# Loading the first group's keys, queries and values amid the projections, and later groups' keys and values in parts

## The chip, the cores and the metric

The kernel runs on one core of one Trainium2 chip. The metric is the device time of one execution in microseconds (us); lower is better. The core has five engines with a queue of their own: PE (TensorE, matmuls), DVE (VectorE), ACT (ScalarE), POOL (GpSimd) and SP (SyncE, which here only issues DMA requests). DMA requests are carried out by 16 DMA engines.

## The reference

Two layers on a graph with 2708 nodes and 128 features. The first layer is an attention with 128 "dimensions" d, each with its own 2708 x 2708 score matrix of inner size 8; the adjacency matrix is added twice to the scores. The second layer is a two-step graph convolution. Both are followed by a residual addition and a layer norm.

```python
q = (x @ Wq.T).reshape(d, n, h)          # d = 128, n = 2708, h = 8
k = (x @ Wk.T).reshape(d, n, h)
v = (x @ Wv.T).reshape(d, n, h)
a = einsum('dnh,dmh->dnm', q, k) * d**-0.5 + adj + adj
out = einsum('dnm,dmh->dnh', softmax(a, axis=2), v).reshape(n, h * d) @ Wo.T
x = layernorm(x + out)
hid = adj @ (x @ W2) + b2
x = layernorm(x + adj @ (hid @ W4) + b4 + hid @ res_w.T + res_b)
```

## The kernel before

The work has three stages, one after the other.

**Projections** (lines 179 to 210). The 2708 rows of x go in 22 chunks `MC` of 128 (the last has 20). For each chunk and each of k, q, v, PE makes a 128 x 1024 product in PSUM (`pp`). ACT copies it to an SBUF tile, for k and q as a rounded high part (`pr`, pool of 4), and DVE adds the low part (line 206) and two reductions for a later range test (line 210). SP then stores the tile into DRAM: `ks` and `qs` (line 208, 1 MB each, in runs of 512 bytes) and `vs` (line 201, 0.5 MB). The reshape of the reference makes one of the 128 dimensions a run of 2708 positions in these DRAM tensors; so the loop reads back from DRAM what the projections wrote. The inputs are requested in the order x, weights of k, q, v (lines 185 and 189).

**Attention loop** (lines 213 to 443). The 128 dimensions go in 32 groups of `GB` = 4. A group needs:

- its keys: `load_keys` (line 276) makes 16 requests of 8 rows of 2708 numbers each (84.6 KB) into `k_raw`, which has one buffer; `order_keys` (line 286) has POOL put them in order in 8 casts (line 291) and 4 small ones (line 295), into a tile with two buffers;
- its values: `load_values` (line 297) makes 4 requests for `v_raw` and 4 small ones for `v_short`; `spread_values` (line 306) has POOL spread them in 4 copies;
- its queries, by block of 452 columns: `load_q` (line 310), 8 requests.

Each group runs over 6 blocks `QBS` of query columns, and each block over 9 steps of a `plan`. A step makes its scores on PE (`score`, line 350), DVE adds an adjacency tile to them (`add_near`, line 357), and ACT takes the exponential of the step's 4 to 8 score tiles at once (line 443). For nine of the key chunks, the exponential of the adjacency is multiplied on POOL instead of added (lines 440 and 441). PE sums exponentials times values into `acc` (`add_up`, line 371). When a block's sum is complete, DVE copies it and SP stores it (`hand_on`, lines 377 and 379).

Adjacency tiles come from DRAM on SP's queue (`load_adj`, line 319): `col` (pool of 9), `two` (a pair of chunks, pool of 3) and `ecol` (exponentials, pool of 7; in group 0 ACT makes them on line 338 and SP stores them on line 339). At each step's beginning the program asks for what is needed up to `ahead` = 8 loads beyond that step.

The order of all this is written out by hand: the generator `interleave` yields pieces, sums and hand-overs, and `tc.manual_schedule()` keeps that order on every engine's queue. The projections lie ahead of the manual schedule; there the order follows from the framework's scheduler. SP's queue is strict: a request that waits (for a buffer, or for data) holds up all that come after it. What asks for a next group's data is these lines:

```python
if (b, i) == (1, 0):
    load_keys(g + 1)
elif (b, i) == (2, 0):
    load_values(g + 1)
elif b > 1 and n % 2:
    h = ((b - 2) * len(plan) + i) // 2     # order_keys(g+1, h), then spread_values
```

For group 0, all of it stands ahead of the loop (lines 385 to 391): `load_keys(0)`, `load_values(0)`, `load_q(0, 0)`, then `order_keys` and `spread_values`. The tiles of the loop lie in SBUF where the projections' tiles were.

**The rest** (from line 446): output projection, layer norm, the range test and the graph convolution. The change does not touch it.

Of the kernel before, what the change touches and what calls it, by code (L numbers as in the profile page):

```python
# [9 lines left out]
F32 = mybir.dt.float32  # L10
# [8 lines left out]
P = 128  # L19
H = 8  # L20
# [109 lines left out]
def graph_attention_gcn(ctx: ExitStack, tc: tile.TileContext, x, xT, adj, adjT, adjP, adjS,  # L130
# [46 lines left out]

    with ExitStack() as s:
        wpool = s.enter_context(tc.tile_pool(name="wqkv", bufs=1))
        sb = s.enter_context(tc.tile_pool(name="proj", bufs=4))  # L180
        ps = s.enter_context(tc.tile_pool(name="ps_proj", bufs=4, space=PSUM))

        xT_sb = wpool.tile([P, N], F32, name="xT_sb")
        for i0, mi in ((0, P), (P, N - P)):
            nc.sync.dma_start(xT_sb[:, ds(i0, mi)], xT[:, ds(i0, mi)])
        w_sb = []
        for name, w in (("k", WkT), ("q", WqT), ("v", WvT)):
            t = wpool.tile([P, H * P], F32, name=f"w{name}_sb")
            nc.sync.dma_start(t, w)
            w_sb.append(t)  # L190
        v3 = vs.rearrange("(i g) e -> i (g e)", g=P)
        for c, (i0, mi) in enumerate(MC):
            for w, dst in zip(w_sb, (ks, qs, vs)):
                pp = ps.tile([P, 2, 512], F32, tag="pp", name="pp")
                for h in range(2):
                    nc.tensor.matmul(pp[:mi, h, :], xT_sb[:, ds(i0, mi)], w[:, ts(h, 512)], start=True, stop=True)
                flat = pp[:mi].rearrange("p a b -> p (a b)")
                if dst is vs:
                    o = sb.tile([P, H * P], F32, tag="po", name="po")
                    nc.scalar.copy(o[:mi], flat)  # L200
                    nc.sync.dma_start(v3[ds(i0, mi)], o[:mi])
                else:
                    f = half_scale if dst is qs else 1.0
                    o = sb.tile([P, 2, H * P], F32R, tag="pr", name="pr")
                    nc.scalar.mul(o[:mi, 0], flat, f)  # L205
                    nc.vector.scalar_tensor_tensor(o[:mi, 1], flat, f, o[:mi, 0].bitcast(F32), ALU.mult, ALU.subtract)
                    d3 = dst.rearrange("e (i g) -> i e g", g=P)
                    nc.sync.dma_start(d3[ds(i0, mi)], o[:mi].bitcast(F32).rearrange("p l (e g) -> p (l e) g", g=P))
                    for i, op in enumerate((ALU.max, ALU.min)):
                        nc.vector.tensor_reduce(ends[:mi, int(dst is qs), i, c : c + 1], o[:mi, 0].bitcast(F32), AX.X, op)  # L210


    with ExitStack() as s:
# [7 lines left out]
        epool = s.enter_context(tc.tile_pool(name="weights", bufs=4))  # L221
        ppool = s.enter_context(tc.tile_pool(name="products", bufs=4))
        opool = s.enter_context(tc.tile_pool(name="sums", bufs=2))
        ps = s.enter_context(tc.tile_pool(name="ps_s", bufs=2, space=PSUM))
        pq = s.enter_context(tc.tile_pool(name="ps_q", bufs=1, space=PSUM))
        pa = s.enter_context(tc.tile_pool(name="ps_a", bufs=1, space=PSUM))
# [49 lines left out]
        def load_keys(g):  # L276

            t = raw.tile([P, N], F32R, tag="k_raw", name="k_raw")
            for j in range(GB):
                r0 = (GB * g + j) * N  # L280
                for i in range(4):
                    nc.sync.dma_start(t[ds(32 * j + H * i, H), :].bitcast(F32), ks[ds(H * (i // 2), H), ds(r0, N)])
            groups[g] = kpool.tile([P, NU, P], F32R, tag="k", name="k"), k_short[g % 2], vals[g % 2], v_short[g % 2]
            raw_keys[g] = t
# [12 lines left out]
        def load_values(g):  # L297
            t = raw.tile([P, GB, NU * H], F32, tag="v_raw", name="v_raw")
            vz = v_short[g % 2]
            for j in range(GB):  # L300
                r0 = (GB * g + j) * N
                nc.sync.dma_start(t[:, j, :], vs[ds(r0, P * NU), :].rearrange("(p c) e -> p (c e)", c=NU))
                nc.sync.dma_start(vz[ds(32 * j, SHORT), ds(VW * j, H)], vs[ds(r0 + P * NU, SHORT), :])
            values[g] = t
# [14 lines left out]
        def load_adj(n):  # L319
# [6 lines left out]
            elif m < 0 and g > 0:  # L326
                t = exp_cols[g, b, -1 - m] = ecols.tile([P, QB], F32, tag="ecol", name="ecol")
                nc.sync.dma_start(t[:, :nw], near_exp[b, -1 - m][:, :nw])
            else:
                t = adj_cols[g, b, m] = cols.tile([P, QB], F32, tag="col", name="col")  # L330
                m = -1 - m if m < 0 else m
                nc.sync.dma_start(t[:, :nw], adjP[ds(m * P, P), ds(n0, nw)])

# [50 lines left out]
        ahead, loaded = 8, 0  # L384
        load_keys(0)
        load_values(0)
        load_q(0, 0)
        for h in range(9):
            order_keys(0, h)
        for j in range(GB):  # L390
            spread_values(0, j)
        for what, n, c, beside in interleave(plan, len(steps) // len(plan), NU):
# [10 lines left out]
            if c == 0:  # L403
# [4 lines left out]
                if g + 1 < NG:  # L408
                    if (b, i) == (1, 0):
# [302 lines left out]
```

## Time and profile before

| | |
|---|---|
| median of 3 runs | 7141.34 us (7120.3 to 7145.82) |
| profiled execution: time | 7152.27 us |
| profiled execution: span from first to last instruction | 7150.5 us |
| mean granted TensorE clock | 0.981 |
| busy: PE, DVE, ACT, POOL | 95%, 86%, 92%, 80% |
| last projection store has landed, first key request | 204.74 us |
| ACT's first large exponential of the loop | 238.17 us |

The profile is of one execution. Busy time is the time in which an engine has an instruction of the program in work; the DMA share is the mean busy share of the 16 DMA engines. Times are microseconds from the first instruction, and L443 means line 443 of the kernel. In the table of groups of instructions, each row ends with busy time and mean ns of one, then the engine's idle time just before them and what ended most of it. In a timeline a row has start, duration, engine, line, operation, destination<-source and count; rows of "SPq" are DMA requests on SP's queue, and their duration is the issuing alone (a merged row runs from the first to the last of its requests).

### The profile page before, as it was taken

To read this page: it belongs to the slowest core of one execution; us is meant where nothing else is said; L and a number is where in the kernel's file an instruction comes from. 1 tells how busy PE (TensorE), PEld (TensorE's weight loads), DVE (VectorE), ACT (ScalarE), POOL (GpSimd) and SP (SyncE) were. 2 spreads that over 40 slices of the span, in tenths; PEclk is the share of its full clock that TensorE was granted. 3 is DMA by queue.
4 is the path that set the end of the run, shared out by engine and by line. 5 is a ranking of instruction groups with operands and counts; after the bars stand their busy time and mean duration, and the time that the engine had idled before them with its cause. 6 is when DMAs were issued, how large, how long until landed. Compare 5 with 4: busy or idle time off the path is not lost. (4 is left out here: it accounts for less than half of the span.)

```text
span 7150.5 us, 136834 instructions
## 1 busy us (share of the span) xinstructions
PE 6813.9 (95%) x50426; PEld 2184.1 (31%) x50426; DVE 6156.5 (86%) x6292; ACT 6560.1 (92%) x3710; POOL 5755.0 (80%) x2525
## 2 busy tenths in 40 slices
PE   6599999999999999999999999999999999999979
PEld 2122233223332332222222332332322232323354
DVE  7589899989998998898899998998989998989831
ACT  3699999999999999999999999999999999999810
POOL 0578888888888888888888888888888888888625
PEclk9799999999999999999999999999999999999979
DMA  9776767767766767776677677677667767766647
GB/s 288 223 245 231 231 224 242 234 221 241 232 226 228 244 222 226 235 239 220 219 239 232 224 242 235 221 237 232 223 222 242 234 222 232 245 222 222 202 151 238
DMA packets 1101142, 1642.67 MB, mean 230 GB/s; under 512 B 144516, under 2 KB 1078804, under 8 KB 1096236
## 3 DMA queue, kind: packets, MB, share of 16 engines
q1 hardware_dynamic: 1081260, 1575.13, 67.7%
q0 software_dynamic: 19200, 58.68, 2.4%
q8 instruction: 399, 6.54, 0.4%
q14 instruction: 283, 2.32, 0.1%
HBM read 1551.44 MB, written 81.80 MB: 228 GB/s over the span
## 5 line engine op out<-in xcount | busy, mean ns | idle before, releaser
L441 POOL TENSOR_TENSOR w<-w,ecol 128x1356 f32<-128x1356 f32 (+1 forms) x1728 | 5351.6, 3104 | 925.2 <-ACT w L440 837.6
L357 DVE TENSOR_TENSOR e<-s,col 128x904 f32<-128x904 f32 (+1 forms) x4608 | 4830.4, 1092 | 483.9 <-PE s L350 172.7
L443 ACT ACTIVATE e<-e 128x2712 f32<-128x2712 f32 (+5 forms) x1728 | 4707.8, 2724 | 2.7 <-DVE e L357 2.5
L371 PE MATMUL acc<-e,vals 128*32 128x452 f32 x21888 | 3839.4, 557 | 11.4 <-ACT e L443 0.6
L350 PE MATMUL s<-q,k 32*128 32x452 f32 x10944 | 2464.1, 468 | 191.3 <-DVE e L357 80.6
L440 ACT ACTIVATE w<-p 128x1356 f32<-128x1356 f32 (+1 forms) x1728 | 2396.3, 1387 | 72.2 <-PE p L350 64.4
L350 PEld LDWEIGHTS s<-q,k 32*128 32x128 f32 x10944 | 1025.7, 182 | 3358.0 <-DVE e L357 2833.3
L371 PE MATMUL acc<-w,vals 128*32 128x452 f32 x10368 | 1670.2, 558 | 0.0
L350 PE MATMUL p<-q,k 32*128 32x452 f32 (+1 forms) x5184 | 1272.7, 439 | 12.3 <-ACT w L440 12.1
L357 DVE TENSOR_TENSOR e<-s,two 128x904 f32<-128x904 f32 (+1 forms) x960 | 1048.2, 1092 | 191.0 <-ACT w L440 82.6
L371 PEld LDWEIGHTS acc<-e,vals 128*32 128x32 f32 x21888 | 621.2, 108 | 855.0 <-issue 787.5
L350 PEld LDWEIGHTS p<-q,k 32*128 32x128 f32 x5184 | 521.2, 183 | 30.7 <-ACT w L440 30.1
L371 PEld LDWEIGHTS acc<-w,vals 128*32 128x32 f32 x10368 | 280.2, 108 | 205.1 <-issue 179.6
L558 POOL DMA_DIRECT2D col<-in_adjT x264 | 141.3, 537 | 231.9 <-SPq L539 159.2
L291 POOL CAST k<-k_raw 128x336 fp32r<-128x336 f32 x256 | 226.3, 886 | 15.1 <-DMA v_short<-vs 15.1
L367 PE MATMUL acc<-e,v_short 128*128 128x452 f32 (+1 forms) x384 | 196.7, 594 | 0.0
L233 POOL MEMSET k_short<- 128x128 f32 x2 | 0.3, 205 | 203.4 <-DMA vs<-po 203.4
L205 ACT ACTIVATE pr<-pp 128x1024 fp32r<-128x1024 f32 (+1 forms) x44 | 45.0, 1024 | 112.4 <-DMA ks<-pr 52.5
L377 DVE COPY o<-acc 128x452 f32<-128x452 f32 x192 | 118.5, 617 | 6.2 <-PE acc L371 6.2
L474 ACT ACTIVATE sd<-mv,eps 128x1 f32<-128x1 f32 (+1 forms) x44 | 12.5, 293 | 120.5 <-DVE mv L472 118.4
L559 PE MATMUL acc<-col,xw 128*128 128x512 f32 (+2 forms) x264 | 106.3, 556 | 9.8 <-DMA col<-in_adjT 9.8
L571 ACT COPY hw<-ph 128x128 f32<-128x128 f32 (+1 forms) x22 | 5.4, 266 | 115.3 <-PE ph L570 115.3
(73 smaller groups left out, 1251.0 us busy)
## 6 DMA issues: line engine op xcount, KB each, us to landing
col<-in_adjP SPq DMA_DIRECT2D x1965, 226.0 KB
two<-in_adjP SPq DMA_DIRECT2D x1440, 226.0 KB
ecol<-ne SPq DMA_DIRECT2D x1395, 226.0 KB
col<-in_adjP SPq DMA_DIRECT2D x393, 224.0 KB
two<-in_adjP SPq DMA_DIRECT2D x288, 224.0 KB
ecol<-ne SPq DMA_DIRECT2D x279, 224.0 KB
col<-in_adjT POOLq DMA_DIRECT2D x210, 256.0 KB, 4.5
k_raw<-ks SPq DMA_DIRECT2D x512, 84.6 KB
```

Source lines behind the costliest of these rows:

```text
L205: nc.scalar.mul(o[:mi, 0], flat, f)
L291: nc.gpsimd.tensor_copy(k[:, :, ts(i, n)], t[:, ts(i, n * NU)].rearrange("p (q c) -> p c q", c=NU))
L350: nc.tensor.matmul(to[:, :nw], k[r, m, :], q[r, :nw], start=True, stop=True)
L357: nc.vector.tensor_add(e[:, ds(at, 2), :nw], st[:, :, :nw], a)
L367: nc.tensor.matmul(a[:, :nw], vz, e[:, t, :nw], start=False, stop=False)
L371: nc.tensor.matmul(a[ds(32 * j, VW), :nw], v[:, m, ds(VW * j, VW)], e[:, t, :nw], start=(m == first_chunk), stop=(m == last_chunk))
L377: nc.vector.tensor_copy(o[:, :nw], acc.pop((g, b))[:, :nw])
L440: nc.scalar.activation(w[:, :, :nw], sp[:, :, :nw], AF.Exp, scale=2.0)
L441: nc.gpsimd.tensor_mul(w[:, :, :nw], w[:, :, :nw], exp_cols[g, b, two][:, :nw].unsqueeze(1).to_broadcast([P, 3, nw]))
L443: nc.scalar.activation(e[:, :at, :nw], e[:, :at, :nw], AF.Exp, scale=2.0)
L558: nc.gpsimd.dma_start(t[:mw, :nw], adjT[ds(m0, mw), ds(n0, nw)])
L559: nc.tensor.matmul(acc[:, :nw], src[:mw, m, :], t[:mw, :nw], start=(m == 0), stop=(last is None and m == NM - 1))
```

## The change

The two stages change their order in the program, and the requests for keys and values are cut in parts.

- The pools and constant tiles that the first group needs are made ahead of the projections; the pools `weights`, `products`, `sums` and the loop's PSUM pools come after them.
- The inputs of the projections are requested in another order: the first 128 columns of xT, the three weights, then the rest of xT.
- After the projections of row chunk 3, the program asks for the first group's keys, first queries and values, and for the first 8 adjacency loads; after those of row chunk 6 it puts keys and values in order. In the built program SP's queue has the inputs, four adjacency requests, the stores of chunks 0 to 3, then 16 requests for keys, 8 for queries, 8 for values, 5 for adjacency, and then the stores of chunk 4 and on. POOL's constant fills come at the program's start.
- For later groups, `load_keys(g, h)` makes two of the 16 requests, and is called at the steps 0 to 7 of block 1; `load_values(g, j)` makes two of the 8, at the steps 0, 2, 4 and 6 of block 2. The steps at which POOL orders keys and spreads values stay the same.

```diff
-        def load_keys(g):
-
-            t = raw.tile([P, N], F32R, tag="k_raw", name="k_raw")
-            for j in range(GB):
-                r0 = (GB * g + j) * N
-                for i in range(4):
-                    nc.sync.dma_start(t[ds(32 * j + H * i, H), :].bitcast(F32), ks[ds(H * (i // 2), H), ds(r0, N)])
-            groups[g] = kpool.tile([P, NU, P], F32R, tag="k", name="k"), k_short[g % 2], vals[g % 2], v_short[g % 2]
-            raw_keys[g] = t
+        def load_keys(g, h):
+
+            if h == 0:
+                groups[g] = kpool.tile([P, NU, P], F32R, tag="k", name="k"), k_short[g % 2], vals[g % 2], v_short[g % 2]
+                raw_keys[g] = raw.tile([P, N], F32R, tag="k_raw", name="k_raw")
+            for i in (2 * h, 2 * h + 1):
+                nc.sync.dma_start(raw_keys[g][ds(H * i, H), :].bitcast(F32),
+                                  ks[ds(H * (h % 2), H), ds((GB * g + h // 2) * N, N)])
...
-        def load_values(g):
-            t = raw.tile([P, GB, NU * H], F32, tag="v_raw", name="v_raw")
+        def load_values(g, j):
+            if j == 0:
+                values[g] = raw.tile([P, GB, NU * H], F32, tag="v_raw", name="v_raw")
             vz = v_short[g % 2]
-            for j in range(GB):
-                r0 = (GB * g + j) * N
-                nc.sync.dma_start(t[:, j, :], vs[ds(r0, P * NU), :].rearrange("(p c) e -> p (c e)", c=NU))
-                nc.sync.dma_start(vz[ds(32 * j, SHORT), ds(VW * j, H)], vs[ds(r0 + P * NU, SHORT), :])
-            values[g] = t
+            r0 = (GB * g + j) * N
+            nc.sync.dma_start(values[g][:, j, :], vs[ds(r0, P * NU), :].rearrange("(p c) e -> p (c e)", c=NU))
+            nc.sync.dma_start(vz[ds(32 * j, SHORT), ds(VW * j, H)], vs[ds(r0 + P * NU, SHORT), :])
...
+        ahead = 8
...
             xT_sb = wpool.tile([P, N], F32, name="xT_sb")
-        for i0, mi in ((0, P), (P, N - P)):
-            nc.sync.dma_start(xT_sb[:, ds(i0, mi)], xT[:, ds(i0, mi)])
+            nc.sync.dma_start(xT_sb[:, :P], xT[:, :P])
             (weights of k, q, v)
+            nc.sync.dma_start(xT_sb[:, P:], xT[:, P:])
...
             for c, (i0, mi) in enumerate(MC):
                 (projections of chunk c as before)
+                if c == 3:
+                    for h in range(2 * GB):
+                        load_keys(0, h)
+                    load_q(0, 0)
+                    for j in range(GB):
+                        load_values(0, j)
+                    for n in range(ahead):
+                        load_adj(n)
+                elif c == 6:
+                    for h in range(9):
+                        order_keys(0, h)
+                    for j in range(GB):
+                        spread_values(0, j)
...
         s.enter_context(tc.manual_schedule())
-        ahead, loaded = 8, 0
-        load_keys(0)
-        load_values(0)
-        load_q(0, 0)
-        for h in range(9):
-            order_keys(0, h)
-        for j in range(GB):
-            spread_values(0, j)
+        loaded = ahead
...
                 if g + 1 < NG:
-                    if (b, i) == (1, 0):
-                        load_keys(g + 1)
-                    elif (b, i) == (2, 0):
-                        load_values(g + 1)
-                    elif b > 1 and n % 2:
+                    if b == 1 and i < 2 * GB:
+                        load_keys(g + 1, i)
+                    elif b == 2 and i % 2 == 0 and i < 2 * GB:
+                        load_values(g + 1, i // 2)
+                    if b > 1 and n % 2:
                         h = ((b - 2) * len(plan) + i) // 2
```

## The prediction

> **What bounds the kernel now.** I read the page's shares first, then the costliest groups, then busy time by stretch, and only then SP's queue around the two places that the change touches.
>
> ```profile
> PE 6813.9 (95%) x50426; PEld 2184.1 (31%) x50426; DVE 6156.5 (86%) x6292; ACT 6560.1 (92%) x3710; POOL 5755.0 (80%) x2525
> ...
> L443 ACT ACTIVATE e<-e 128x2712 f32<-128x2712 f32 (+5 forms) x1728 | 4707.8, 2724 | 2.7 <-DVE e L357 2.5
> ```
>
> Four engines are above 80%, so the shares don't settle it; ACT's exponentials hardly ever wait (2.7 us over 1728). The stretches settle it (columns: stretch and its length, busy time of PE, PEld, DVE, ACT and POOL, PE clock, DMA share, GB/s):
>
> ```profile
> 0.00:204.74 204.74, 127.74 (x264) 47.95 (x264) 151.74 (x132) 67.09 (x67) 0.81 (x7) 0.93 0.91 286
> 204.74:226.48 21.74, 0.00 (x0) 0.00 (x0) 0.00 (x0) 0.00 (x0) 6.14 (x14) 0.50 0.52 78
> 226.48:238.17 11.69, 3.42 (x13) 1.53 (x13) 4.15 (x5) 1.80 (x2) 9.26 (x17) 0.50 0.67 206
> 272.00:322.00 50.00, 35.61 (x243) 9.89 (x241) 29.01 (x29) 36.91 (x26) 27.43 (x9) 0.80 0.82 219
> 1721.60:1771.60 50.00, 49.47 (x387) 15.11 (x379) 45.93 (x47) 50.00 (x28) 42.11 (x15) 1.00 0.79 257
> 2729.60:2779.60 50.00, 45.11 (x336) 13.63 (x339) 40.37 (x41) 44.56 (x25) 36.59 (x13) 0.93 0.79 218
> 2779.60:2829.60 50.00, 49.26 (x389) 15.05 (x393) 45.70 (x46) 50.00 (x29) 47.12 (x21) 1.00 0.67 220
> 238.17:6640.00 6401.83, 6239.27 (x47999) 1905.32 (x47999) 5774.39 (x5649) 6317.59 (x3443) 5495.10 (x2191) 0.99 0.71 231
> ```
>
> There are three regimes. The projections (to 204.74) are bound by DMA. From 204.74 to 238.17 nearly everything waits. The attention loop is bound by ACT, which is full in the ordinary stretch 2779.6 to 2829.6. In the whole loop ACT is idle for 6401.83 - 6317.59 = **84.2 us**. The stretches of 50 us that begin at each of the 31 requests for the next group's keys hold 81.5 of these: 13.1 in the first (at 272), 68.4 in the other thirty. These differ: 0.0 at 1721.6, 5.4 at 2729.6. From request to request the group at 709.1 comes 206.5 us after that at 502.6, the one at 1920.9 only 199.3 after that at 1721.6.
>
> SP's queue at the loop's start and at one later group (start, us, line, transfer), and the two other engines at the start:
>
> ```profile
> 204.74 11.87 SPq L282 DMA_DIRECT2D k_raw<-ks  x16
> 226.63 3.55 SPq L315 DMA_DIRECT2D q<-qs  x8
> 230.22 1.37 SPq L332 DMA_DIRECT2D col<-in_adjP  x3
> ...
> 226.48 6.63 POOL L291 CAST k<-k_raw 128x336 fp32r<-128x336 f32 x8 [15.15 <-DMA v_short<-vs]
> 238.17 3.22 ACT L443 ACTIVATE e<-e 128x3616 f32<-128x3616 f32 x1 [0.88 <-DVE e L357]
> ...
> 502.60 11.06 SPq L282 DMA_DIRECT2D k_raw<-ks  x16
> 514.08 0.35 SPq L332 DMA_DIRECT2D col<-in_adjP  x1
> ...
> 521.75 2.25 SPq L379 DMA_DIRECT2D os<-o  x4
> 524.34 4.54 SPq L315 DMA_DIRECT2D q<-qs  x8
> ```
>
> At the start: the last store lands at 204.7, then keys, values and queries are requested, POOL orders the keys (226.5 to 233.1), and the first large exponential runs at 238.17: 33.4 us. Later: sixteen key requests hold SP for 11 us, adjacency columns wait behind them, and 8 us on come the sums and next queries, which take another 6.7. In the waits between 2720 and 2765 the victim is named:
>
> ```profile
> DVE e L357 <- DMA col<-in_adjP: 4.6, 1, 4.6
> ```
>
> [...] DMA share 0.52 while keys alone move. [...] the trace has 78 GB/s, so I use 78 for keys that move alone.
>
> **Part 1, the first group amid the projections.** In the built program's order on SP, sixteen key requests, eight for queries, eight for values and the rest of eight adjacency loads follow the stores of the fourth row chunk; POOL's casts follow on. Everything goes through SP's one queue, ahead of the stores of chunk 5. So in a DMA-bound stage it isn't free: I count DMA time.
> - Filled: between 10 and 20 us the DMA share is 0.47, 5.3 us idle. The new order asks for 128 columns of x and the weights first, and puts four adjacency requests behind the inputs, so DMA work reaches into this gap: -5.3 (0 if it doesn't).
> - Added: nine adjacency requests (eight tiles) of 226 KB are 2.03 MB, at the 296 GB/s of 20 to 200 us: +6.9.
> - Added: queries and values (0.23 and 0.34 MB) are 2 us of transfer, but their 16 small requests keep the engines half empty: +4 (2 to 6).
> - Added: keys, 1.39 MB on half of the engines. If those run at their usual rate, 1.39 MB / 148 GB/s = 9.4; at 78 GB/s, 17.8; with waiting 21.7, as before. I take **+14**, [...].
>
> Last store: 204.7 - 5.3 + 6.9 + 4 + 14 = 224.3 (217.7 to 239.3 with every bound). Tiles of the loop lie where the projections' tiles were, so the first exponential (1.3 us, pitch 1.2) follows this store, the large one about 1.2 later: 225.5 against 238.17, **-12.7** (-19 to +2). A wait on SP holds up the stores behind it; then the four `pr` tiles fill and ACT, DVE and PE wait, as they do now on store landings. Nothing here costs engine time: the casts (6.63 + 0.90 + 1.13) and memsets (6.6) go to POOL, busy 0.81 us of the first 204.7; one exponential of 0.58 moves to ACT, busy 67.1 of these. Were the casts late, PE's first scores would be.
>
> **Part 2, keys in parts.** The count stays 16 + 8 requests a group. Two key requests now stand before the columns of each of eight steps of block 1, and a pair for values before every second step of block 2. A step is some 3.8 us (35 us for nine). A pair holds SP 2 x 0.65 = 1.3 us (11.06/16 is 0.69; 9.1 to 13.5 us in other groups) and eight engines 2 x (10832 x 8 B / 78 GB/s = 1.1) = 2.2 us at worst. Columns, pairs and exponentials of the adjacency are 31 requests a block, at 0.6 us in the dense stretches 2.1 us a step: 2.1 + 1.3 = 3.4 is under 3.8, so lateness doesn't build up. Three pairs stand before the block's sums, where SP waits anyway for DVE's copy (1209 us in 156 waits, 7.7 each): hidden. The tight place is just after it. In the block from 1154 (no keys), the copy ends at 1163.7, requests resume at 1169.9, a pair of columns asked for until 1171.2 is used by DVE at 1176.2; with the 3.8 us that the loop's first columns took (asked for at 230.2, DVE goes at 234.0) 1.2 us are spare, and ACT takes up this step 0.9 us after DVE's end. Against these 2.1 us stand one key pair's 1.3 to 2.2. Requests made 5 us later have 8 us and more to spare. So I expect nearly all of the idle time to go: 76 of 84.2, leaving 0.2 us per group and a little more for the first, where SP also waits for ACT before each of nine stores of exponentials. The bounds are 40, and 84.2. Key casts at block 2, step 1 now follow the last pair by three steps, 11 us, not by some 25; if that pair is late, POOL's multiplications queue behind the cast, then the sums on PE; I take 0.
>
> **Sum.** 12.7 + 76 = 88.7. Against the profiled execution 7152.3 that gives 7063.6. It stands 11 us above the median of the three runs, so the forecast is 7141.3 - 88.7 = **7053**.
>
> **Rivals.**
> 1. *Lateness only moves* (chance 0.15): [...] os, queries and one more pair come together just where 2.1 us are spare. For it: at 2729.6 the idle time appears together with the queries, not at the keys. Against it: blocks with values (eight requests in a row) show no idle time. Half of the 81.5 stays, and the start gives 5 to 12: 7141 - 41 - 9 = 7091.
> 2. *The pairs become a wait in every step* (0.07, the slower end): a pair behind the queries isn't covered, and each of the five pairs after the sums delays DVE's columns by its 1.3 us on SP: 6.3 x 31 = 195 us, less the 84 and 12 gained: 7141 + 99 = 7240. It decides from 97/31 = 3.1 us of uncovered time a group, two and a half pairs. Against it: 3.4 us of requests fit into 3.8.
> 3. *It doesn't do what it says* (0.05): the first key request waits for the fourth chunk's stores, or the projections grow by all that is moved, and ACT's idle time has another cause than the keys: 7141. Against it: the built order shows the parts where the text puts them, and the idle time sits at 31 key requests.
>
> **How the numbers follow.** The main case has 0.73. Its range is 7036 (84.2 and 19, and a few us of run-to-run) to 7085. Rival 1 reaches to some 7105, where I end the range; rivals 2 and 3 lie outside. About 0.5% (36 us) is what a measurement of this kernel can tell from no change: faster takes the main case and most of rival 1, 0.85; same, the rest of it and rival 3, 0.08; slower, 0.07.
>
> **What would show it.** Right: the last store of the projections lands at 220 to 230 and the large exponential starts within 2 us of it; key casts lie before that on POOL; ACT is full in the 50 us after each first pair; the groups' period is near 200 us. Wrong: the last store after 236 (part 1 gives nothing); DVE waiting for columns or pairs in every block 1, or POOL's multiplications behind a cast (part 2).

## The result, and the profile after

The changed kernel takes 7237.53 us (median of 4 runs, 7211.38 to 7245.74), the kernel before 7143.58 us in the same comparison (7120.3 to 7150.55): a ratio of 1.0129, 95% interval 1.0104 to 1.0153. It is slower by 94 us; forecast was 7053.

The page of the changed kernel, shares and then groups (columns as before: busy, mean ns | idle before, releaser):

```profile
PE 6849.1 (95%) x50426; PEld 2173.0 (30%) x50426; DVE 6153.0 (85%) x6292; ACT 6570.9 (91%) x3710; POOL 5754.9 (80%) x2525
...
L449 ACT ACTIVATE e<-e 128x2712 f32<-128x2712 f32 (+5 forms) x1728 | 4678.9, 2708 | 8.2 <-DVE e L370 7.5
...
L446 ACT ACTIVATE w<-p 128x1356 f32<-128x1356 f32 (+1 forms) x1728 | 2367.5, 1370 | 174.2 <-PE p L363 163.9
```

The same engines are as busy as before, and the big exponential (L449) still hardly waits. The wait sits on the other exponential, L446: 174.2 us of idle time, against 72.2 on the same line of the kernel before:

```profile
L440 ACT ACTIVATE w<-p 128x1356 f32<-128x1356 f32 (+1 forms) x1728 | 2396.3, 1387 | 72.2 <-PE p L350 64.4
```

It names PE's scores `p`, but PE itself is late there because DVE is, and DVE because of a transfer. The waits of the changed kernel (us in total, times, longest) show that chain:

```profile
ACT w L446 <- PE p L363: 163.9, 88, 14.6
...
PE s L363 <- DVE e L370: 144.0, 159, 11.1
...
DVE e L370 <- DMA col<-in_adjP: 118.9, 77, 5.4
```

In the kernel before, the last of these lines reads:

```profile
DVE e L357 <- DMA col<-in_adjP: 73.5, 20, 38.0
```

The 38.0 is one wait, at the loop's start; in the loop itself 35.5 us in 19 waits have become 118.9 in 77. The whole loop, from the first to the last large exponential, in the stretches of both kernels (the first line is of the changed kernel, the second of the kernel before):

```profile
233.06:6860.12 6627.06, 6402.24 (x48929) 1942.12 (x48929) 5879.85 (x5755) 6450.22 (x3508) 5596.73 (x2224) 0.98 0.75 227
```

```profile
238.17:6761.85 6523.68, 6359.12 (x48929) 1941.66 (x48929) 5883.11 (x5755) 6439.43 (x3508) 5596.67 (x2224) 0.99 0.71 231
```

The loop has grown by 6627.06 - 6523.68 = 103.4 us. ACT's idle time in it went from 84.2 to 6627.06 - 6450.22 = **176.8 us**; that is 92.6 of the 103.4. The loop starts 5.1 us earlier, and what follows the loop, which the change does not touch, took 12.2 us less in this trace (376.5 us against 388.7; in the 20 traces of this case it varies between these two). In sum 103.4 - 5.1 - 12.2 = 86.1, the difference of the two spans (7236.6 and 7150.5).

The DMA share of the loop rises from 0.71 to 0.75 while GB/s fall from 231 to 227: the same bytes take longer. One later group shows where. First SP's queue with the key pairs of block 1, then stretches of the same time (their length, then busy PE, PEld, DVE, ACT, POOL, PE clock, DMA share, GB/s):

```profile
1112.94 0.91 SPq L240 DMA_DIRECT2D k_raw<-ks  x2
...
1128.30 1.38 SPq L392 DMA_DIRECT2D os<-o  x4
1129.78 5.12 SPq L271 DMA_DIRECT2D q<-qs  x8
1134.94 0.66 SPq L240 DMA_DIRECT2D k_raw<-ks  x2
...
1150.75 0.89 SPq L240 DMA_DIRECT2D k_raw<-ks  x2
```

```profile
1112.00:1115.00 3.00, 3.00 (x29) 0.91 (x27) 2.86 (x3) 3.00 (x2) 2.89 (x1) 1.00 1.05 389
1115.00:1130.00 15.00, 14.89 (x118) 4.73 (x120) 13.82 (x14) 15.00 (x10) 11.85 (x4) 1.00 0.93 214
...
1137.50:1160.00 22.50, 18.13 (x125) 4.88 (x122) 15.81 (x16) 17.93 (x9) 15.34 (x5) 0.91 1.01 204
```

Just before the keys travel, the DMA engines are full at 389 GB/s. With a key pair in nearly every step they are nearly or quite as full (shares 0.93 and 1.01), at 214 and 204 GB/s: what fell is not their busy time but what they get done in it. ACT is idle for 22.50 - 17.93 = 4.6 us of the last stretch, in two waits. The second runs over the end of the stretch, and DVE's wait for a column stands ahead of it:

```profile
1157.28 3.11 DVE L370 TENSOR_TENSOR e<-s,col 128x904 f32<-128x904 f32 x3 [2.73 <-DMA col<-in_adjP]
...
1161.12 1.30 ACT L446 ACTIVATE w<-p 128x1356 f32<-128x1356 f32 x1 [4.01 <-PE p L363]
```

The records of single packets, which the trace also holds, point the same way. I call a packet of 1808 bytes a column packet: one row of an adjacency tile (a few per cent are rows of queries and of sums). In the changed kernel it takes 88 ns on average when no key packet is in flight, and 148 ns when one is. In the kernel before, the two means are 85 and 145 ns; but there only 10,165 column packets start while keys are in flight, since the burst of sixteen requests leaves few columns beside it. In the changed kernel it is some 50,600.

The start, in the changed kernel's DVE queue and ACT queue:

```profile
228.91 4.12 DVE L370 TENSOR_TENSOR e<-s,col 128x904 f32<-128x904 f32 x4 [9.12 <-DMA vs<-po]
```

```profile
233.06 3.22 ACT L449 ACTIVATE e<-e 128x3616 f32<-128x3616 f32 x1 [0.83 <-DVE e L370]
```

The last store landed at 228.9, and the large exponential came at 233.06 where it had come at 238.17.

### The profile page after: what moved, and what is told of

Its sections match the earlier page's. It is cut to its first block, busy times and chain, and to the rows that moved or that the text cites. A ratio compares the mean times of both kernels' runs of the same rounds, so it can differ in the third digit from the quotient of the medians.

```text
span 7236.6 us, 136857 instructions
## 1 busy us (share of the span) xinstructions
PE 6849.1 (95%) x50426; PEld 2173.0 (30%) x50426; DVE 6153.0 (85%) x6292; ACT 6570.9 (91%) x3710; POOL 5754.9 (80%) x2525
## 5 line engine op out<-in xcount | busy, mean ns | idle before, releaser
L449 ACT ACTIVATE e<-e 128x2712 f32<-128x2712 f32 (+5 forms) x1728 | 4678.9, 2708 | 8.2 <-DVE e L370 7.5
L446 ACT ACTIVATE w<-p 128x1356 f32<-128x1356 f32 (+1 forms) x1728 | 2367.5, 1370 | 174.2 <-PE p L363 163.9
L320 DVE SCALAR_TENSOR_TENSOR pr<-pp,pr 128x1024 fp32r<-128x1024 f32 (+1 forms) x44 | 53.7, 1221 | 68.0 <-ACT pr L319 67.3
```

Of the source, the lines that this page charges most:

```text
L446: nc.scalar.activation(w[:, :, :nw], sp[:, :, :nw], AF.Exp, scale=2.0)
L449: nc.scalar.activation(e[:, :at, :nw], e[:, :at, :nw], AF.Exp, scale=2.0)
```

## The experiments

Each was timed against the kernel before, on the same chip. "Idle" is the time in which ACT was not busy between 250 and 6500 us of the trace, 6250 us less its busy time there: 83.5 in the kernel before and 167.6 in the changed one.

| run | what it has | ratio to before, 95% interval | us | idle |
|---|---|---|---|---|
| changed kernel | both parts | 1.0129 (1.0104 to 1.0153) | 7237.5 | 167.6 |
| e1_start_only | part 1 alone | 0.9993 (0.9976 to 1.001) | 7134.6 | 79.3 |
| e2_parts_only | part 2 alone | 1.0123 (1.0074 to 1.0172) | 7228.2 | 172.4 |
| e3_short_keys | key rows of 32 numbers | 0.9869 (0.9823 to 0.9915) | 7041.4 | 0.2 |
| e4_no_keys | no later key requests | 0.987 (0.9824 to 0.9916) | 7042.5 | 0.5 |
| e5_halves | two bursts of 8 | 0.9886 (0.987 to 0.9903) | 7053.8 | 10.0 |
| e6_pairs_clear | pairs in other steps | 1.0024 (1.0011 to 1.0037) | 7155.3 | 110.5 |
| e7_rows16 | 16 rows a request | 0.9877 (0.986 to 0.9893) | 7046.9 | 3.7 |
| e8_wide | 128 short rows | 0.9871 (0.9855 to 0.9888) | 7040.4 | 0.3 |
| e9_wide_7 | 119 rows, overlapping | 1.0437 (1.0419 to 1.0455) | 7446.6 | 353.4 |
| e10_rows16_all | 16 rows, complete | 0.9895 (0.9878 to 0.9913) | 7063.0 | 16.7 |
| e11_halves_old_start | two bursts, old start | 0.9908 (0.9891 to 0.9925) | 7070.8 | 9.1 |
| e12_wide_119 | 119 short rows | 0.9859 (0.9837 to 0.9882) | 7042.1 | 2.0 |
| e13_wide_126 | 126 short rows | 0.9853 (0.9831 to 0.9875) | 7040.2 | 0.3 |
| e14_pieces | 8 rows in short pieces | 1.0208 (1.0184 to 1.0232) | 7293.8 | 243.8 |
| e15_rows21 | 21 rows of 4 KB | 0.9878 (0.9858 to 0.9898) | 7056.5 | 19.0 |
| e16_one_run | 8 rows read from one place | 1.012 (1.008 to 1.0161) | 7233.7 | 184.2 |
| e17_spread_rows | 8 rows, four partitions apart | 0.9877 (0.9849 to 0.9905) | 7049.3 | 8.9 |
| e18_spread_all | spread keys and queries, complete | 0.9988 (0.9974 to 1.0001) | 7133.4 | 83.1 |

**Which part is it?** e1 is the changed kernel with the later groups' keys and values asked for at once again; e2 is the kernel before with the later requests in parts.

```diff
-                    if b == 1 and i < 2 * GB:
-                        load_keys(g + 1, i)
-                    elif b == 2 and i % 2 == 0 and i < 2 * GB:
-                        load_values(g + 1, i // 2)
+                    if (b, i) == (1, 0):
+                        for h in range(2 * GB):
+                            load_keys(g + 1, h)
+                    elif (b, i) == (2, 0):
+                        for j in range(GB):
+                            load_values(g + 1, j)
```

> Only the first part of the change: the start as in the changed kernel, later groups' 16 key requests at once at step 0 of block 1 and their 8 value requests at once at step 0 of block 2, as before. The first large exponential came 5.1 us earlier in the changed kernel (233.06 against 238.17). If the loss sits in the parts (theory A: key transfers that run beside column transfers slow both), this kernel is 5 us faster than before: about 7138, ACT idle in the loop near the 84 us of before. If the start costs something that the two marks don't show (rival: tiles or buffers that now lie elsewhere in SBUF), it is slower than before, up to all of the 94 us.

> Only the second part: the start as before, later groups' keys and values in parts. Theory A: all of the loss and none of the 5 us gained, about 7143 + 94 + 5 = 7242, ACT idle in the loop near 177 us. Rival (the start's new places in SBUF): near 7143.

Part 2 alone carries the loss: e2 is at 1.0123 with 172.4 us of idle time. Part 1 alone lies between 17 us faster and 7 slower, which can't be told from no change, though its trace has the large exponential at 226.13, 12.0 us earlier than before.

**SP's time or the data?** e3 makes every request as before, in the same steps, but with rows of 32 numbers instead of 2708 for the later groups; e4 leaves these requests out. The later groups then work on keys that aren't theirs. (In these two, in e8, e9 and in e12 to e17, later groups also keep the first group's key tile instead of a new one.)

```diff
...
-                nc.sync.dma_start(raw_keys[g][ds(H * i, H), :].bitcast(F32),
-                                  ks[ds(H * (h % 2), H), ds((GB * g + h // 2) * N, N)])
+                w = N if g == 0 else 32
+                nc.sync.dma_start(raw_keys[g][ds(H * i, H), :w].bitcast(F32),
+                                  ks[ds(H * (h % 2), H), ds((GB * g + h // 2) * N, w)])
```

> The changed kernel with the same number of key requests at the same places in SP's queue, but for later groups each row of a key request is 32 numbers long instead of 2708 (the other keys stay those of the first group, so these groups' results are left out). Theory A (the data of keys beside columns): the stall in block 1 vanishes; ACT idle in the loop falls from 177 to under 20 us, about 7075. Rival B (SP's slots: 16 more requests, five pairs of them after the block's sums, hold up the columns whatever they carry): the stall stays, 150 us or more of idle time, 7210 or more. The mix of both would lie between and give the share of each.

> The changed kernel without any key request for later groups (they use the first group's keys, so their results are left out); POOL still puts keys in order. It gives the floor: what the loop takes if keys cost no DMA at all. Theory A and rival B both: ACT idle under 15 us, about 7143 - 5 - 75 = 7063. If idle time of 40 us or more stays, part of it doesn't come from keys but from values, queries or sums.

The requests of e3 hold SP as long as those of the changed kernel: 0.31 us each, on average over the loop, in both traces. The pair behind the queries, in e3:

```profile
1096.04 0.76 SPq L241 DMA_DIRECT2D k_raw<-ks  x2
```

Yet the idle time is 0.2 us, and the stretch that answers to 1137.50 to 1160.00 above (the same 22.5 us, from 2.56 us after the pair behind the queries) reads:

```profile
1098.60:1121.10 22.50, 22.31 (x176) 6.82 (x172) 20.34 (x21) 22.50 (x12) 18.41 (x7) 1.00 0.96 312
```

ACT is full and the engines move 312 GB/s. So the sixteen requests in pairs cost nothing as such; the loss, and the 84 us of the kernel before too, come with the bytes of the keys. e4, without the requests, is the floor: 7042.5.

**Where the pairs stand.** My first account was that the five pairs after the block's queries do the harm. e6 puts the pairs into steps away from them.

```diff
+        PAIRS = [(0, 0), (0, 1), (0, 2), (0, 7), (0, 8), (1, 0), (1, 1), (1, 2)]
...
-                    if b == 1 and i < 2 * GB:
-                        load_keys(g + 1, i)
+                    if b < 2 and (b, i) in PAIRS:
+                        load_keys(g + 1, PAIRS.index((b, i)))
```

> Eight pairs as in the changed kernel, but none in the steps 3 to 6 that follow a block's sum: at steps 0, 1, 2, 7 and 8 of block 0 and 0, 1, 2 of block 1. Theory A1 (a pair always slows the DMA, but only those behind the sum and the queries stall ACT, where the columns have no spare time): ACT idle falls from 168 to some 20 us, about 7060. Rival A2 (the DMA time lost in eight pairs, some 11 us of all engines a group, is too much wherever they stand): 100 us or more stay, 7150 or above.

110.5 us stay: the place takes off a third only. That account fell. The idle time isn't beside the pairs, either. In 29 of the groups the last key packet has landed 0.5 to 1.5 us before the first query request of that block, and of 107 us of idle time in them 104 come 5 to 20 us after that request. One group, first with its pairs and then behind its queries:

```profile
1101.00:1118.00 17.00, 16.90 (x136) 5.22 (x135) 15.87 (x16) 17.00 (x10) 14.21 (x5) 1.00 0.91 201
1122.50:1137.50 15.00, 12.47 (x83) 3.37 (x79) 9.61 (x10) 10.71 (x6) 9.30 (x4) 0.77 0.88 291
```

With the pairs ACT is full although DMA moves only 201 GB/s; it is idle 4.3 us afterwards, behind the queries, when DMA is fast again. So pairs away from the queries cost too, and what they cost shows up later, at the place that has the least time to spare.

**Bursts.** e5 keeps the new start and asks for the keys in two bursts of eight, at the first steps of blocks 0 and 1; values at once. It is a complete kernel. e11 is the same with the old start.

```diff
...
+                    if b < 2 and i == 0:
+                        for h in range(GB * b, GB * b + GB):
+                            load_keys(g + 1, h)
...
```

> Keys of later groups in two bursts of 8 requests, at step 0 of blocks 0 and 1 (before: one burst of 16; changed kernel: 8 pairs); values at once at step 0 of block 2; the start as in the changed kernel. Theory A (keys are cheap in a burst, when hardly any column moves beside them, and dear in pairs between columns): a burst of 8 takes some 5 us, less than the 7.7 us in which SP waits for the block's sum anyway, so hardly any idle time stays: ACT idle under 15 us in the loop, about 7055. Rival D (each place where keys meet columns costs something, so two places cost more than one): idle time like before or more, 7135 or above.

> Keys in two bursts of 8 at blocks 0 and 1 as in the kernel with two bursts (7054), but with the start as before the change. It prices the start where the loop doesn't stall: by the marks of the two profiles the start is worth 5 us, so 7059; 7054 or less if its earlier end is given back, 7066 if it was worth the 12.7 us of the forecast.

e5 beats both kernels: 7053.8, 1.1% under the kernel before, and is the best complete version here. Eight requests hold SP for some 6.5 us instead of 11, and in the records some 18,400 column packets start beside keys, against 50,600 with pairs. The number alone doesn't decide, though: e6 has 73,100 and loses less than the changed kernel. By the ratios e11 is some 16 us slower than e5; in their traces the large exponential comes at 249.46 and 234.27, both late for their kind of start: with both, the first burst for the next group stands at the loop's first step.

**Key packets at a time.** In the changed kernel's records, 8 key packets or fewer are in flight for 99.5% of the time in which any is; a request has 8 rows. On which engines they move the trace does not show. The eight engines that the prediction counts for a key request can only be estimated from the DMA share of 0.52 in the stretch of before that has keys and values alone: 0.52 x 16 = 8.3. e7 asks for 16 rows at a time, one request per step (the products of high and low parts are left out); e10 does the same and keeps all products by asking for the queries in 12 requests a block.

```diff
-            for i in (2 * h, 2 * h + 1):
-                nc.sync.dma_start(raw_keys[g][ds(H * i, H), :].bitcast(F32),
-                                  ks[ds(H * (h % 2), H), ds((GB * g + h // 2) * N, N)])
+            nc.sync.dma_start(raw_keys[g][ds(2 * H * h, 2 * H), :].bitcast(F32),
+                              ks[:, ds((GB * g + h // 2) * N, N)])
```

> As the changed kernel, same places and bytes, but a key request has 16 rows instead of 8, one request per step instead of two (the low and high parts lie in another order for that, so products of high with low parts are left out). Theory P (8 rows sit on half of the DMA engines and on few partitions): [...] the time in which columns are slowed halves; ACT idle falls from 168 to 40 to 90 us, about 7140. Rival L (long packets, 10.8 KB each, between the columns' 1.8 KB are the cause, on however many engines): little changes, idle 130 us or more, 7190 or above.

> The changed kernel with key requests of 16 rows, one per step, and nothing left out: the second half of each dimension's query rows is loaded as low then high part by two requests of 8 rows instead of one of 16, so each block has 4 more query requests just behind the block's sum. Since requests as such cost nothing (short keys), about the 7047 of the kernel with 16 rows, at most 7065; rival: the four 8-row query requests of 14 KB slow the columns as the 8-row key requests did, 7080 to 7140.

Sixteen rows nearly end the loss, more than either number expected of e7. Yet a column packet beside its keys takes 145 ns, nearly as long as the 148 of the changed kernel, and there are 43,700 of them: that single packets get slower isn't by itself what costs the time. But a request of 16 rows also fills 16 partitions at once, and in all its keys are in flight for 551 us instead of 710. The wide forms nearly keep the bytes, and keep the rhythm, with other shapes: 128, 126 or 119 rows of 169 numbers (86.5, 85.2 and 80.4 KB), read from one run in DRAM (the key tile holds other numbers than the reference's; so it does in e9, e14, e15 and e16).

```diff
...
+                    p, w = 119, 169
+                    nc.sync.dma_start(raw_keys[g][:p, ts(i, w)].bitcast(F32),
+                                      ks[i, ds(min(GB * g * N, R - p * w), p * w)].rearrange("(p c) -> p c", c=w))
```

> As the changed kernel, same places, 16 requests of the same bytes, but for later groups a key request is a block of 128 rows of 169 numbers, shaped like a column request (what lands is not the keys in their places, so these groups' results are left out). If the shape of the request is the cause (theory P or L), 86.5 KB cost no more than 0.4 of a column request and the stall vanishes: ACT idle under 15 us, about 7050. If the bytes themselves are (rival A2), it stays: over 100 us of idle time, 7170 or above.

> As the kernel with wide key requests (128 rows of 169 numbers, no stall), but with 119 rows of 182 numbers, the same 86.6 KB. [...] (What lands is not the keys in their places, so later groups' results are left out.) If half the engines are the cause [...], the stall comes back: ACT idle 80 us or more, 7120 or above. If the few partitions of 8 rows are the cause, it stays away: under 20 us, about 7045 to 7055.

> Key requests of 119 rows of 169 numbers (80.4 KB), one beside the other in SBUF, so that, unlike in the kernel with 119 rows of 182, no request waits for the one before (there SP waited 843 us for this). Later groups' results are left out as there. [...] If half the engines are the cause of the stall, ACT idle is 80 us or more, 7120 or above; if few partitions are, under 20 us, 7040 to 7055.

> The same with 126 rows (85.2 KB)[...]. It is the control: rows, bytes and shape are nearly those of 119. If the number of engines matters, it is like 128 rows, ACT idle under 10 us, 7040 to 7050; if a number of rows that is no power of two is what costs, it is as slow as 119 rows.

e9 says nothing: its rows were 182 wide and lay 165 apart, so each request waited for the one before, as its SP waits show:

```profile
SPq L245 <- DMA k_raw<-ks: 842.8, 383, 4.9
```

e12 is e9 without the overlap. Its key packets are mostly no more than 7 at a time in the records, those of e13 (126 rows) up to 15. Both are at the floor, with 2.0 and 0.3 us of idle time. So few key packets at a time are not by themselves the cause.

**Packet length, reading side, partitions.** e14 keeps 8 rows and cuts each into 16 pieces of 676 bytes; e15 has 21 rows of 4 KB; e16 keeps the 8 rows of 10.8 KB and reads them from one run in DRAM instead of 8 places.

```diff
...
+                    nc.sync.dma_start(raw_keys[g][ds(H * i, H), :].bitcast(F32),
+                                      ks[i, ds(min(GB * g * N, R - H * N), H * N)].rearrange("(p c) -> p c", c=N))
```

> The changed kernel with the later groups' key requests still over 8 partitions and 86.5 KB, but each row taken in 16 pieces of 169 numbers (676 B) instead of one long run; start, rhythm and bytes as in the changed kernel, and the key tile holds other numbers than the reference's. Theory F (few partitions: eight partitions written beside the columns block the columns' transfers whatever the packet's length): the ScalarE idle time stays near 150 to 180 us and the time near 7220. Theory L (long packets on half of the engines hold the columns back): short packets free it, idle under 20 us, 7045.

> The changed kernel with the later groups' key requests over 21 partitions with rows of 1,024 numbers (4 KB, 86 KB in all)[...]; otherwise as the changed kernel, and the key tile holds other numbers than the reference's. Theory F (few partitions): with 21 partitions the stall is mostly gone, as with 16 rows, idle under 30 us and 7050. Theory L (long packets on half of the engines): [...] idle 80 to 170 us, 7120 to 7220.

> The changed kernel with the later groups' key requests writing 8 partitions as before, but reading one contiguous run of 86.7 KB in DRAM instead of 8 runs 1.4 MB apart; the key tile holds other numbers than the reference's. Theory D (what counts is how many partitions are written): the stall stays, ScalarE idle 150 to 250 us, 7210 to 7300. Theory S (what counts is the reading from 8 far rows, as in e14_pieces, while the wide forms and e15_rows21 read one run): the stall goes, idle under 20 us, 7045.

Short pieces make it worse (243.8 us idle), 21 rows nearly end it (19.0), and reading from one place changes nothing (184.2): the same stretch of e16 reads 198 GB/s at a full share.

```profile
1130.90:1153.40 22.50, 19.45 (x129) 5.47 (x125) 15.83 (x16) 18.40 (x10) 15.48 (x5) 0.85 1.01 198
```

What is left is the writing side. e17 changes the place of the rows in the changed kernel: the eight rows of a later key request lie four partitions apart instead of side by side (key rows then meet other query rows than in the reference). Its theory P is the guess that the place of the rows counts.

```diff
-                raw_keys[g] = raw.tile([P, N], F32R, tag="k_raw", name="k_raw")
+                raw_keys[g] = raw.tile([P, N], F32R, tag="k_raw", name="k_raw") if g == 0 else raw_keys[0]
...
-                nc.sync.dma_start(raw_keys[g][ds(H * i, H), :].bitcast(F32),
+                at = ds(H * i, H) if g == 0 else ds(32 * (i // 4) + i % 4, H, step=4)
+                nc.sync.dma_start(raw_keys[g][at, :].bitcast(F32),
                                   ks[ds(H * (h % 2), H), ds((GB * g + h // 2) * N, N)])
```

> The changed kernel with one thing different: the later groups' key requests write 8 partitions four apart instead of 8 neighbours (the same reading, bytes, packets, engines and rhythm; key rows then stand beside other query rows than the reference pairs). [...] Theory P [...]: the stall goes, ScalarE idle under 20 us, 7045. Theory N (the number of partitions written, wherever they lie): the stall stays, idle 150 to 190 us, 7230.

The stall is gone: 8.9 us idle, 7049.3. (That the key tile is kept isn't the reason: e14 and e16 keep it and stall.) The stretch has 282 GB/s, and its pairs even hold SP longer than those of the changed kernel:

```profile
1105.97:1128.47 22.50, 21.84 (x172) 6.81 (x172) 19.87 (x20) 22.22 (x12) 18.27 (x6) 1.00 0.97 282
```

```profile
1103.41 1.33 SPq L241 DMA_DIRECT2D k_raw<-ks  x2
```

Same bytes, packets, rows in a request, reading and steps as the changed kernel, and eight partitions in both: what decides is which partitions are written. The packet records give, for the time in which key packets of later groups are in flight (the rate counts all packets that start in that time), in the order of the rate:

| run | partitions that one request writes | time with keys in flight, us | all DMA in that time, GB/s | idle, us |
|---|---|---|---|---|
| e14_pieces | 8 neighbours | 826 | 174 | 243.8 |
| changed kernel | 8 neighbours | 710 | 190 | 167.6 |
| e16_one_run | 8 neighbours | 714 | 192 | 184.2 |
| e6_pairs_clear (other steps) | 8 neighbours | 819 | 215 | 110.5 |
| e7_rows16 | 16 neighbours | 551 | 223 | 3.7 |
| e15_rows21 | 21 neighbours | 653 | 248 | 19.0 |
| e17_spread_rows | 8, four apart | 529 | 266 | 8.9 |
| e12_wide_119 | 119 neighbours | 566 | 271 | 2.0 |
| e13_wide_126 | 126 neighbours | 481 | 288 | 0.3 |
| e8_wide | all 128 | 433 | 310 | 0.3 |

Among neighbours the rate rises with the number of partitions: 174 to 215 GB/s with 8, 223 with 16, 248 with 21, 271 to 310 with 119 and more (with 21 and more the packets are shorter, too). Yet eight partitions four apart have 266, more than 21 neighbours, so their number alone doesn't set it. The loop moves 231 GB/s on average before, and 235 in e13, at the floor: with 8 neighbours the rate stays short of that as long as keys travel, with 16 it comes near, and in the rows below it is above. That holds for requests spread over the steps; the bursts of e5, over 8 neighbours too, go at 169 GB/s and leave 10.0 us. The idle time doesn't follow the rate in every row: e15 at 248 GB/s has more of it than e7 at 223, and e6 at 215 has 110.5 us where e7 has 3.7. Where between them the loss begins, and why, was not tested. Nor do the runs show what columns wait for when keys go to eight neighbours; they show that the place of the rows decides: 167.6 us of idle time side by side, 8.9 four apart.

**A complete version with spread rows.** e18 spreads the keys four apart and the queries two apart, so that their rows pair as the reference wants, and stores the query rows in that order.

```diff
+                at = ds(32 * (h // 2) + h % 2 + 2 * (i % 2), H, step=4)
+                nc.sync.dma_start(raw_keys[g][at, :].bitcast(F32),
...
-                    nc.sync.dma_start(q[ds(32 * j + 2 * H * i, 2 * H), :nw].bitcast(F32),
+                    nc.sync.dma_start(q[ds(32 * j + i, 2 * H, step=2), :nw].bitcast(F32),
```

> A complete version of the changed kernel, nothing left out: key requests write 8 partitions four apart and query requests 16 partitions two apart, with the query rows stored in DRAM in the matching order (two stores a chunk instead of one). Theory P: idle under 10 us; 7040 to 7055, at the floor of the run without later key requests (7042) and at or under the two-burst version (7054). Theory N: 7230.

It missed: 7133.4, 83.1 us idle, though with keys in flight it moves 266 GB/s as e17 does. Of 74 us of idle time in 29 groups, 50 stand in the block of the keys, most of them 15 to 20 us after its first query request, 13 in the block after it, and 2 to 3 in each of the others. DVE waits for the columns of a pair, which it hardly did in e17 (16.0 us):

```profile
DVE e L376 <- DMA two<-in_adjP: 118.7, 143, 3.4
```

What differs from e17 ahead of that place is the query requests, which stand in every block: in the group shown eight hold SP for 6.08 us where e17's took 4.72 (on average over the loop 5.3 and 3.9).

```profile
1081.25 6.08 SPq L272 DMA_DIRECT2D q<-qs  x8
```

```profile
1098.64 4.72 SPq L272 DMA_DIRECT2D q<-qs  x8
```

1.4 us more stand there against the 2.1 us spare that I had worked out. That this is the cause was not tested by itself; how the queries are written, and how they are stored at the start, differs as well.

## Why the prediction was wrong

**What bounds the loop: right.** ACT is the bound, keys are what makes it idle, and the room is what I took it to be: with no key requests idle time is 0.5 us and the time 7042.5. That two bursts gave 7053.8, the forecast almost to the microsecond, is a coincidence: it is another arrangement than the one I forecast.

**Part 1: the mark was right, by two errors that cancel; its worth isn't measured.** I predicted the last store at 224.3 and the large exponential at 225.5. In the 16 traces with this start (the changed kernel and all experiments but e2, e11 and e18) the large exponential starts between 224.8 and 234.3, median 226.7; three traces with the old start have 237.6, 238.2 and 249.5. The changed kernel's own trace, 233.06, is one of the late ones. What the earlier start is worth in time can't be told from nothing (e1). The terms: the gap filled as I said (DMA share 1.02 from 10 to 20 us, where it was 0.47), and the stretches at the keys, then at queries and values, are in part empty as I said (0.65 and 0.51):

```profile
10.00:20.00 10.00, 10.00 (x25) 4.41 (x24) 9.75 (x9) 6.25 (x8) 0.00 (x0) 1.00 1.02 316
44.37:59.50 15.13, 10.81 (x20) 4.23 (x20) 6.95 (x6) 3.27 (x4) 0.38 (x2) 0.89 0.65 140
59.50:73.00 13.50, 0.00 (x0) 0.00 (x0) 0.00 (x0) 0.00 (x0) 6.55 (x9) 0.52 0.51 111
```

The queries and values were sized too small, 4 us (2 to 6): their requests alone take SP from 59.49 to 70.09, in a stretch in which the engines are half empty and PE, DVE and ACT stand still. What I left out is that DVE's four adds, 4.12 us, also wait for the last store, so that the large exponential follows it by 4.15 us and not by 1.2. Against that, the store itself lands earlier than my sum in most traces: at 222.6 in the median of the 16 (220.7 to 230.1). Which term made the sum too large is open; the 14 us for the keys were an estimate between the 9.4 and 21.7 us given beside them.

**Part 2: wrong, by this step.** "2.1 + 1.3 = 3.4 is under 3.8, so lateness doesn't build up." It counts SP's time to issue, and e3 shows that this costs nothing. For the engines it counts the pair's own duration, 2.2 us "at worst", and takes the columns beside it at the rate they have alone. The pair's duration wasn't too small: a key packet takes 0.89 us on average, two in a row 1.8. What is missing is the columns. The trace of before has the keys nearly alone on the engines, since the burst keeps the columns behind it; I had no row for keys and columns together, and put what they do to each other at nothing. Measured: with key pairs the stretch runs at 204 GB/s where the same work without the keys' bytes moves 312, and a column packet beside a key packet takes 148 ns instead of 88. So cutting the burst in pieces takes away what had kept it from meeting the columns: 402 us with keys in flight became 710, with five times as many column packets beside them. The lateness does build up, and comes out behind the queries, as in e6.

The bounds of the main case for the idle time that goes, 40 to 84.2, left out a loss; in the loop it was -92.6. The sign that I had named shows it: ACT was to be full in the 50 us after each first pair, and in these 31 stretches it is idle for 142.3 us, 2.4 us or more in every one (81.5 before).

**The rivals.** The number of rival 2, 7240, is what came out, but by luck, not by its mechanism: it priced 1.3 us of SP's time per uncovered pair, and e3 has all the pairs and no loss. (Five times 1.3 is 6.5, not 6.3; its sum would be 7247.) Its other half, that pairs become a wait in the steps after the sums, is what the waits show. Rival 1 named the tight place, and it is real: it is where the idle time of e6 comes out, though no pair stands there, so lateness does move. But a pair there is not the cause of it, and eight rows a request are not (e17 has them too). Rival 3 is out: the change did what it says.

**The rate of keys alone.** The 78 GB/s come from a stretch that also holds values; the first group's keys by themselves took 19.3 us in flight, 72 GB/s. In the bursts of before 43.0 MB of keys took 402 us in flight, 107 GB/s, with 8 key packets or fewer in flight for 99.6% of that time. What I priced was keys alone; that few of their packets are in flight at a time turned out harmless by itself (e12, 2.0 us idle). What counts is what they do to the transfers beside them.

## What to carry to other kernels

Here a burst that held SP for some 11 us cost less than its pieces (83.5 us of idle time against 167.6): it ran nearly alone, with 10,165 column packets beside its keys against some 50,600. Before cutting a burst in pieces, ask what each piece does to the transfers that it will now run beside, and look for a stretch in the trace where both are in flight. A full DMA share with falling GB/s was the sign of such a clash (1.01 at 204 GB/s, against 0.96 at 312 without the keys' bytes): read the two columns together. Look for the idle time later than the cause, too: in e6, 104 of 107 us came 5 to 20 us after the first query request, where the schedule had the least to spare, though the last key packet had landed before it. Where a load fills few partitions, try other ones: eight rows four apart instead of side by side took the idle time from 167.6 to 8.9 us, while shorter packets (243.8) and another way of reading (184.2) did not help.

## What the runs showed of the hardware

- A load into 8 neighbouring partitions slowed the loads into 128 partitions beside it (changed kernel): 148 ns instead of 88 per 1808-byte packet, and 190 GB/s in all while it lasted, at a full DMA share (204 GB/s at 1.01 in the stretch shown). With its rows four partitions apart the same load left 102 ns and 266 GB/s (e17).
- Sixteen neighbouring rows in one request slowed the packets nearly as much (145 ns), but lasted shorter (551 us in all against 710) at 223 GB/s, and cost next to nothing (e7, 3.7 us idle).
- Cutting the packets from 10,832 to 676 bytes made it worse, not better (e14, 174 GB/s and 243.8 us idle against 190 and 167.6); reading from one place in DRAM instead of eight made no difference (e16, 192 GB/s).
- Requests whose rows lie apart in SBUF held SP longer: 0.65 us a request for 8 rows four apart against 0.31 for 8 neighbours (e17 and the changed kernel), and 0.62 against 0.44 for 16 rows two apart (queries of e18 and e17), on average over the loop.
- A request that waited on SP held up those behind it: before the stores of a block's sum SP waited for DVE's copy, 1208.9 us in 156 waits in the kernel before (9.2 at most), and the queries behind them were requested only then (nothing between 1159.5 and 1163.75 us, then the stores, queries from 1165.23).
